# Six-feature groups on two 32-row blocks, and the side matmuls gathered behind every third slot

## The chip, the core and the metric

One core of a Trainium2 chip runs the whole kernel in one launch. The time is device microseconds of an execution; the kernel before takes 6139.32 us (median of 3 runs, 6136.94 to 6142.77).

## The reference, cut to what matters

The input is 8 images of 128 channels on 36 by 36 pixels. A convolutional attention layer is followed by a layer over tokens, of which the costly part is an additive attention: each image has 1296 tokens of 128 features, and every pair of tokens is scored by a sum of 128 hyperbolic tangents.

```python
q = jnp.einsum('bld,ed->ble', x, Wq) + bq
k = jnp.einsum('bld,ed->ble', x, Wk) + bk
t = jnp.tanh(q[:, :, None, :] + k[:, None, :, :])
scores = jnp.einsum('bijd,d->bij', t, w) + bw[0]
attn = jax.nn.softmax(scores, axis=-1)
return jnp.einsum('bij,bjd->bid', attn, x)
```

A mixture of 64 experts with one hidden layer follows, on the 8 best tokens of each expert. Everything is float32.

## The kernel before, in words

**Scores as fractions.** A tangent is written with exponentials, and the fractions of five or six features are brought to one denominator. Numerator and denominator of such a group are then each a dot product over all sign combinations of its features, 32 for a group of five and 64 for a group of six. The kernel holds exponentials of all these combinations for the queries (`qf`, with a plain and a weighted version) and for the keys (`kf`), in `NF` = 8 blocks of 128 partitions: blocks 0 to 3 hold 16 groups of five, 32 partitions each; blocks 4 to 7 hold 8 groups of six, 64 partitions each. `signs` (L524) builds the matrix of signs at the start, on POOL (L532).

**Units and slots.** A unit is one image (8), one chunk of 432 queries (3) and one tile of 128 keys (10, and an eleventh of 16 keys that works in another layout, `REM_SLOTS`). A full unit has 12 slots of two groups each, listed in `SLOTS` (L50): in every three slots, two of five and then one of six. In all there are 2928 slots.

**One slot** makes two tiles of 128 keys by 432 queries of denominators `d` and two of numerators `n`, each by a matmul over the group's partitions (`products`, L939, the matmul at L949). One float32 matmul has two records in the profile. ACT takes the logarithm of both denominators (L972), and after every second slot one exponential of minus that (L975): this makes reciprocals `lq`. DVE multiplies numerators by them (`terms`, L985, the products at L990 to L1003); in slots 2, 5, 8 and 11 (`DVE_PAIRS`, just the slots of six) DVE also adds them up, in place in PSUM, and otherwise POOL adds them (L1012). At a unit's end POOL joins the two sums and ACT takes the exponential of the score (L1032).

**The order of the loop** (L1113 and on) is written out by hand and each engine runs its instructions in it. In turn `p` it issues the numerators of slot `p`, the denominators of slot `p + 3` (`LAG`), the products of slot `p`, and then a turn of other matmuls. A slot of five uses two of the four 32-row quarters of the TensorE array for `n`, and the slot three later uses the other two for `d`; a slot of six uses two 64-row halves for `n` and then the same two for `d`.

**Buffers.** `d` has two buffers of two PSUM banks (`ps_d`). The other four banks (`ps_n`) go round: two for each slot's numerators and one for each step of a side matmul (`aux`). `qf` has 9 buffers (`qfp`).

**Side work.** Everything else (the next image's convolutions, its first attention, tokens, keys; this image's query blocks, its weighted sum, its gates) is written as generators that yield after each step, in four lanes with a precedence: `first_of_all`, `urgent`, `gates`, `background`. A step that issues matmuls is run by `matmul_turn` (L1077) after a slot's own work, one step in a turn, not after slots 1, 4, 7 and 10 except for the first lane, and within a budget of `PACE` = 400 columns for each slot, saved up to two. The instructions that take its result out of PSUM are the generator's next step; `TAKE` lets them be issued by `take_turns` (L1072) in the next turn, outside slots 2, 5, 8, 11 except for the first lane. The next chunk's query blocks are made in the last unit of a chunk, one after each second and third of three slots, in the order `IN_TURN`.

Of the kernel before, what the change touches and what calls it, by code (L numbers as in the profile page):

```python
# [3 lines left out]

# [6 lines left out]
F32 = mybir.dt.float32  # L11
AF = mybir.ActivationFunctionType
ALU = mybir.AluOpType
# [7 lines left out]
CH = 432  # L21
# [24 lines left out]
NF = 8  # L46
FIVES = 4 * 5 * (NF // 2)

SLOTS = []
for m in range(NF // 2):  # L50
    for i in range(2):
        half = (m + i) % 2
        SLOTS.append((m, [slice(64 * half + 32 * h, 64 * half + 32 * h + 32) for h in range(2)]))
    SLOTS.append((NF // 2 + m, [slice(64 * h, 64 * h + 64) for h in range(2)]))
NP = len(SLOTS)
IN_TURN = [m + i for m in range(NF // 2) for i in (0, NF // 2)]
LAG = 3
SHIFT = 6.5
DVE_PAIRS = (2, 5, 8, 11)
PACE = 400  # L60

HALVES = [slice(0, 64), slice(64, 128)]
REM_BANKS = [[(q + i, rows) for i in range(2) for rows in HALVES] for q in (0, 2)]
REM_BANKS.append([(NF // 2 + i, slice(0, 128)) for i in range(4)])
REM_SLOTS = [REM_BANKS[:2], REM_BANKS[2:]]


@with_exitstack  # L70
def kernel(
# [28 lines left out]
    nc = tc.nc  # L100
    mm = nc.tensor.matmul
    ctx.enter_context(tc.manual_schedule())

    const = ctx.enter_context(tc.tile_pool(name="const", bufs=1))
# [25 lines left out]
    with ExitStack() as loop, ExitStack() as score:  # L130
# [20 lines left out]
        ps_n = pool("ps_n", 4, space=bass.MemoryType.PSUM)  # L151
# [19 lines left out]
        def load_raw_taps(w, name):  # L171
# [36 lines left out]
            out=gavg3, in_=gavg3, compare_op=ALU.is_ge, fill=0.0, base=0,  # L208
# [4 lines left out]
            pattern=[[C // G, G], [0, C // G]], channel_multiplier=-1,  # L213
        )

        pairs = const.tile([128, 2, 2], F32, tag="pairs", name="pairs")
        nc.gpsimd.memset(pairs, 0.0)
        for s in range(2):
            nc.gpsimd.memset(pairs[64 * s : 64 * s + 64, 1, s : s + 1], 1.0)
            for o in (32 * s, 64 + 32 * s):  # L220
                nc.gpsimd.memset(pairs[o : o + 32, 0, s : s + 1], 1.0)

        by_key = const.tile([128, 2, REM], F32, tag="by_key", name="by_key")
        for s in range(2):
# [44 lines left out]

        TAKE = (False, 1)

        def step(rest=1):
            return (False, rest)
# [4 lines left out]
        behind = [0]  # L280
# [241 lines left out]
        def signs():  # L522

            sign = big_tile("sign")[:, : NF * 128]  # L524
            nc.gpsimd.memset(sign, 0.0)
            for n, first, half in ((5, 0, sign[:, : NF * 64]), (6, FIVES, sign[:, NF * 64 :])):
                groups = NF * 64 >> n
                for r in range(n):
                    v = half.rearrange("p (g h b l) -> p g h b l", g=groups, b=2, l=2**r)
                    for bit, value in ((0, -1.0), (1, 1.0)):  # L530
                        w = v[:, :, :, bit, :]
                        nc.gpsimd.affine_select(  # L532
                            out=w, in_=w, compare_op=ALU.not_equal, fill=value, base=-first - r,
                            pattern=[[-n, groups], [0, 2 ** (n - 1 - r)], [0, 2**r]],
                            channel_multiplier=1,
                        )
            return sign

        feat = {}
# [127 lines left out]
        def keys(b, tiles):  # L667

            xT = prepared[b][1]
            yield matmuls(1)  # L670
            for t in tiles:
                o, n = KT[t]
                first = (b, t) == (0, order[0])
                if first:
                    kf_of[0] = kfp.tile([128, NF, 128], F32, tag="kf", name="kf")
                for q0 in (0, NF // 2):
                    some = slice(q0, q0 + NF // 2)
                    pk = aux("pk1").rearrange("p (q t) -> p q t", t=128)
                    for q in range(NF // 2):
                        bmm(pk[:, q, :n], a_k[:, (q0 + q) * 128 : (q0 + q + 1) * 128],  # L680
                           xT[:, o : o + n], start=True, stop=True)
                    yield TAKE
                    if first:
                        ks = kf_of[0][:, some, :]
                    else:
                        ks = kstp.tile([128, NF // 2, 128], F32, tag="ks", name="ks")
                    nc.scalar.activation(ks[:, :, :n], pk[:, :, :n], AF.Exp)
                    kd3 = kd[b][t].rearrange("p (q t) -> p q t", t=128)[:, some, :]
                    if n == REM:

                        for x in range(2):
                            nc.gpsimd.tensor_scalar(
                                ks[:, :, (x + 1) * n : (x + 2) * n], ks[:, :, :n],
                                pairs[:, min(q0, 1), x : x + 1], None, ALU.mult,
                            )
                        nc.sync.dma_start(kd3[:, :, : 2 * n], ks[:, :, n : 3 * n])
                    else:
                        nc.sync.dma_start(kd3, ks)
                    if q0 > 0:
                        made.add((b, t))  # L700
                    yield matmuls()
# [209 lines left out]
        def drain(*gens):  # L911
            for g in gens:
                for _ in g:
                    pass
# [6 lines left out]
        slots = []  # L921
# [15 lines left out]
        def new_block(b, c, q):  # L937
            qf = qfp.tile([128, 2, CH], F32, tag="qf", name="qf")
            qf_of[b, c, q] = qf  # L939
            return query_block(b, c, q, qf)  # L940

        def products(u, k, part, outs):

            b, c, j = units[u]
            kf = kf_of[u]
            if j < NKT - 1:
                q, rows = SLOTS[k]
                for h in range(2):
                    mm(outs[h][:, :CH], kf[rows[h], q, :], qf_of[b, c, q][rows[h], part, :],  # L949
                       start=True, stop=True)  # L950
                return
            for out, bank in zip(outs, REM_SLOTS[k]):
                for i, (q, rows) in enumerate(bank):
                    mm(out[32 * i : 32 * i + 32, :CH], kf[rows, q, :32],  # L954
                       qf_of[b, c, q][rows, part, :], start=True, stop=True)

        def banks(u, k):
            return 2 if units[u][2] < NKT - 1 else len(REM_SLOTS[k])

        def denominators(p):  # L960

            if p >= len(slots):
                return
            u, k = slots[p]
            d = ps_d.tile([128, 2, 512], F32, tag="d", name="d")
            n = banks(u, k)
            products(u, k, 0, [d[:, h, :] for h in range(n)])
            if k % 2 == 0:
                lq_of[u, k // 2] = lp.tile([128, 4, CH], F32, tag="lq", name="lq")
            lq = lq_of[u, k // 2]  # L970
            o = 2 * (k % 2)
            nc.scalar.activation(lq[:, o : o + n, :], d[:, :n, :CH], AF.Ln)  # L972
            if k % 2 == 1:
                some = lq[:, : o + n, :]
                nc.scalar.activation(some, some, AF.Exp, scale=-1.0)  # L975

        def numerators(p):
            ns = [ps_n.tile([128, 512], F32, tag="n", name="n") for _ in range(banks(*slots[p]))]
            products(*slots[p], 1, ns)
            return [ps[:, :CH] for ps in ns]  # L980

        def terms(p, ns):

# [90 lines left out]
                if lane.due(p, False) and (k not in DVE_PAIRS or lane is first_of_all):  # L1074
                    lane.run(p)

        def matmul_turn(p, k):  # L1077


            before = behind[0]  # L1080
            for lane in lanes:
                while lane.due(p, True) and behind[0] == before:
                    paced = balance[0] < 0 or k + 1 in DVE_PAIRS
                    if lane is not first_of_all and paced or lane is gates and urgent:
                        break
                    lane.run(p)
            balance[0] = min(balance[0] - (behind[0] - before) + PACE, 2 * PACE)

        drain(normal(0))
        for name in ("wv_t", "wq_t"):  # L1090
# [9 lines left out]
        a_q, a_k, cs_s, fb_s, eb_s = (feat[n] for n in ("a_q", "a_k", "cs_s", "fb_s", "eb_s"))  # L1100
        drain(tokens(0), keys(0, order[:1]))
        for i, q in enumerate(IN_TURN):
            if i < 3:
                drain(new_block(0, 0, q))
            else:
                first_of_all.append(new_block(0, 0, q))
        for p in range(LAG):
            denominators(p)
        drain(keys(0, order[1:3]))
        prefetch(1)  # L1110
        urgent.append(keys(0, order[3:]))
# [1 line left out]
        for p, (u, k) in enumerate(slots):  # L1113
# [12 lines left out]
                             keys(b + 1, range(NKT)))  # L1126
                        )
            take_turns(p, k)
            ns = numerators(p)
            denominators(p + LAG)  # L1130
            terms(p, ns)
            if pending and pending[0][0] <= p:
                exps(p, *pending.popleft()[1:])
            last = p + 1 == len(slots) or slots[p + 1][0] != u

            if j == order[-1] and u + 1 < len(units) and k % 3:
                used = IN_TURN.index(SLOTS[k][0]) + 1
                if used < NF:
                    first_of_all.append(new_block(*units[u + 1][:2], IN_TURN[used]))
            elif j == order[-2] and last and u + 2 < len(units):  # L1140
                first_of_all.append(new_block(*units[u + 2][:2], IN_TURN[0]))
            matmul_turn(p, k)
            if last and rem:
                first_of_all.append(rem_scores(p, u, live.pop("rem")))
            elif last:
# [212 lines left out]
```

The softmax here doesn't subtract the row's maximum and nothing guards it: scores larger than these inputs give would overflow.

## Time and profile before

| what | value |
|---|---|
| median of the runs | 6139.32 us |
| span of the profiled execution | 6139.0 us |
| around the span (median less span) | 0.3 us |
| first and last logarithm (L972) start | 156.2 and 5983.1 us |
| busy share PE, ACT, DVE, POOL | 97, 86, 78, 75% |
| mean granted TensorE clock | 0.985 of full |
| DMA | 270.87 MB, mean 44 GB/s |

A busy share is the time in which an engine has an instruction in flight, over the span. The profile's pages name TensorE as PE for its matmuls and PEld for its weight loads, VectorE as DVE, ScalarE as ACT, GpSimd as POOL. A window's row gives for each engine the busy time and, in brackets, the number of instructions. A timeline row gives the start, the time to the end of the last of the merged instructions, the engine, the line, the operation, what it writes and reads, and rows by columns of the array. The list of waits gives who waited for whom, the sum in us, how often, and the longest.

The work falls into a head (to 156.2 us) that makes the first image's first attention, tokens and first keys; eight batches of 33 units, one for each image, seven of them with the next image's side work; and a tail of experts from 5985 us on.

### The profile page before, as it was taken

Reading aid. Unit: us, or ns where it says so; the run is one execution under the profiler, and the core shown is the slowest. Engines: PE = TensorE matmul, PEld = TensorE weight load, DVE = VectorE, ACT = ScalarE, POOL = GpSimd, SP = SyncE. Lnnn points to the kernel's source line nnn. Section 1 sums busy time; section 2 is a strip of 40 time slices with the busy share of each in tenths; the row PEclk is TensorE's granted clock in tenths of the full one; section 3 lists DMA queues with packets and bytes.
Section 4 is the critical chain, followed back from the end, with each engine's and each line's share of the span. In section 5 each row is a group of like instructions: output and inputs, shape, how many; then the busy total and the mean of one; then the engine's idle time right before and its main releaser. Section 6 shows DMA issues by size and latency. Waiting matters only on the chain.

```text
span 6139.0 us, 93072 instructions
## 1 busy us (share of the span) xinstructions
PE 5957.9 (97%) x33480; PEld 2862.1 (47%) x33480; DVE 4796.4 (78%) x9521; ACT 5279.9 (86%) x5371; POOL 4597.7 (75%) x2819
## 2 busy tenths in 40 slices
PE   7999999999999999999999999999999999999996
PEld 5454444544544445444455444454444544544443
DVE  4787878877788787877888777887778877788882
ACT  1888898888988888889998889888898888999990
POOL 4777777777787777778778786877777777787870
PEclk9999999999999999999999999999999999999997
DMA  1210011100110002100111001110011100110008
GB/s 44 70 37 22 25 62 38 34 25 28 68 43 20 26 27 71 39 24 23 44 55 39 22 24 59 44 39 22 20 65 40 34 25 28 58 50 29 28 20 297
DMA packets 151519, 270.87 MB, mean 44 GB/s; under 512 B 45648, under 2 KB 76752, under 8 KB 151056
## 3 DMA queue, kind: packets, MB, share of 16 engines
q1 hardware_dynamic: 151056, 264.92, 13.0%
q8 instruction: 264, 4.33, 0.3%
q14 instruction: 199, 1.63, 0.1%
HBM read 200.41 MB, written 64.19 MB: 43 GB/s over the span
## 4 chain that ended last, share of the span: by engine, by line
PE 77%; ACT 7%; DVE 6%; issue 6%; POOL 2%; DMA 1%; SPq 0%; DVEq 0%; POOLq 0%; ACTq 0%
PE n L949 37%; PE d L949 12%; PE pa L284 7%; PE pc L284 5%; ACT lq L972 5%; PE s L284 3%; PE pk L284 3%; PE pq L284 3%; DVE rp L1003 2%; DVE n L997 1%; DVE accd L999 1%; PE d L954 1%; ACT lq L975 1%; DMA w<-in_weight_dram 1%; PE n L954 1%
## 5 line engine op out<-in xcount | busy, mean ns | idle before, releaser
L1012 POOL TENSOR_TENSOR accp<-accp,rp 128x864 f32<-128x864 f32 x1440 | 2915.8, 2025 | 1041.0 <-DVE rp L1003 948.8
L949 PE MATMUL n<-qf,kf 32*128 32x432 f32 (+1 forms) x11520 | 3325.3, 574 | 46.5 <-ACT e L1032 13.3
L949 PE MATMUL d<-qf,kf 32*128 32x432 f32 (+1 forms) x11520 | 2991.6, 561 | 38.7 <-ACT lq L972 38.2
L972 ACT ACTIVATE lq<-d 128x864 f32<-128x864 f32 x2928 | 2524.2, 878 | 542.6 <-PE d L949 512.1
L1003 DVE TENSOR_TENSOR rp<-n,lq 128x432 f32<-128x432 f32 x3912 | 2173.3, 600 | 743.5 <-PE d L949 542.8
L975 ACT ACTIVATE lq<-lq 128x1728 f32<-128x1728 f32 (+1 forms) x1464 | 2398.2, 1638 | 46.3
L949 PEld LDWEIGHTS n<-qf,kf 32*128 32x128 f32 (+1 forms) x11520 | 1206.4, 184 | 1600.3 <-DVE rp L1003 581.5
L949 PEld LDWEIGHTS d<-qf,kf 32*128 32x128 f32 (+1 forms) x11520 | 1090.0, 185 | 422.1 <-issue 224.7
L997 DVE TENSOR_TENSOR n<-n,lq 128x432 f32<-128x432 f32 x1440 | 814.9, 608 | 142.1 <-PE n L949 88.5
L999 DVE TENSOR_TENSOR accd<-n,accd 128x432 f32<-128x432 f32 x1440 | 866.3, 602 | 24.6
L1010 POOL TENSOR_TENSOR accp<-rp 128x864 f32<-128x864 f32 x240 | 485.2, 2022 | 197.7 <-DVE rp L1003 195.6
L711 POOL TENSOR_SCALAR qf<-qf,cs_s 128x432 f32<-128x432 f32 x192 | 260.9, 1365 | 45.0 <-ACT qf L710 44.4
L284 PEld LDWEIGHTS pa<-xh,e 128*108 128x108 f32 x1920 | 222.5, 174 | 131.1 <-DVE rp L1003 56.0
L1021 POOL TENSOR_TENSOR accd<-accp,accd 128x432 f32<-128x432 f32 x240 | 265.2, 1105 | 18.8
L1019 POOL TENSOR_TENSOR accp<-accp 128x432 f32<-128x432 f32 x240 | 264.4, 1102 | 16.7
L284 PE MATMUL pa<-xh,e 128*108 128x129 f32 x1920 | 262.9, 283 | 8.7 <-ACT e L1032 5.2
L284 PE MATMUL s<-q,k 128*116 128x432 f32 x480 | 230.3, 568 | 1.7 <-DVE q L316 1.4
L284 PEld LDWEIGHTS pk<-xT,a_k 128*128 128x128 f32 x1408 | 171.2, 192 | 107.0 <-DVE n L997 33.7
L462 POOL TENSOR_TENSOR tot<-tot,e 116x432 f32<-116x432 f32 x192 | 212.0, 1104 | 6.0 <-ACT e L471 4.6
L471 ACT ACTIVATE e<-s 116x432 f32<-116x432 f32 x240 | 124.9, 520 | 98.3 <-PE s L284 97.9
L284 PE MATMUL pa<-e,vw 116*128 116x432 f32 x480 | 204.6, 549 | 0.0
L284 PE MATMUL pk<-xT,a_k 128*128 128x128 f32 (+1 forms) x1408 | 202.5, 287 | 0.1
(213 smaller groups left out, 3788.4 us busy)
## 6 DMA issues: line engine op xcount, KB each, us to landing
kf<-kd SPq DMA_DIRECT2D x239, 512.0 KB
kd<-ks SPq DMA_DIRECT2D x158, 256.0 KB
w<-in_weight_dram SPq DMA_DIRECT2D x32, 1024.0 KB
wk_t<-wk_t_d SPq DMA_DIRECT2D x7, 768.0 KB
wv_t<-wv_t_d SPq DMA_DIRECT2D x7, 768.0 KB
wq_t<-wq_t_d SPq DMA_DIRECT2D x7, 768.0 KB
x<-in_x_dram SPq DMA_DIRECT2D x8, 648.0 KB
t<-tokd SPq DMA_DIRECT2D x96, 54.0 KB
```

The lines of the kernel that those rows point to most:

```text
L284: mm(out, lhsT, rhs, **kw)
L711: nc.gpsimd.tensor_scalar(qf[:, 1, :], qf[:, 0, :], cs_s[:, q : q + 1], None, ALU.mult)
L949: mm(outs[h][:, :CH], kf[rows[h], q, :], qf_of[b, c, q][rows[h], part, :], start=True, stop=True)
L972: nc.scalar.activation(lq[:, o : o + n, :], d[:, :n, :CH], AF.Ln)
L975: nc.scalar.activation(some, some, AF.Exp, scale=-1.0)
L997: mult(ns[h], ns[h], lq[:, o + h, :])
L999: nc.vector.tensor_add(live["d"], ns[h], live["d"])
L1003: mult(rp[:, h, :], n, lq[:, o + h, :])
L1010: nc.gpsimd.tensor_add(live["p"], live["r"], rp)
L1012: nc.gpsimd.tensor_add(live["p"], live["p"], rp)
L1019: nc.gpsimd.tensor_add(s[:, 0, :], s[:, 0, :], s[:, 1, :])
L1021: nc.gpsimd.tensor_add(d, s[:, 0, :], d)
```

## The change

The groups of six keep their 64 sign combinations, but these now lie in two blocks: the 32 combinations of the first five features and a minus sign for the sixth in one block, and those with a plus sign two blocks on, on the same 32 partitions. A slot of six is now four matmuls of 32 rows for `n` and four for `d`, in pairs that accumulate in PSUM, on the same two quarters; and the generators `numerators` and `denominators` are run in rounds, so that two matmuls of `n` and two of `d` follow each other. The line numbers of the changed kernel are 963 for these matmuls and 290 for the side matmuls.

`matmul_turn` gives the paced lanes a turn only after slots 2, 5, 8 and 11, and then runs as many steps as a budget of 355 columns for each slot (saved up to four) allows; `TAKE` becomes (False, 0), and the step that takes a result out is issued at once in the same turn. The first lane may still run after any slot. The next chunk's query blocks are ordered after the new use of blocks and made after slots 2, 5, 8 (two) and 11 (two), the last after slot 2 of the new chunk.

```diff
-    for i in range(2):
-        half = (m + i) % 2
-        SLOTS.append((m, [slice(64 * half + 32 * h, 64 * half + 32 * h + 32) for h in range(2)]))
-    SLOTS.append((NF // 2 + m, [slice(64 * h, 64 * h + 64) for h in range(2)]))
+    for blocks, half in (
+        ((m,), m % 2),
+        ((m,), (m + 1) % 2),
+        ((NF // 2 + m // 2, NF // 2 + 2 + m // 2), m % 2),
+    ):
+        rows = [slice(64 * half + 32 * h, 64 * half + 32 * h + 32) for h in range(2)]
+        SLOTS.append((blocks, rows))
...
-IN_TURN = [m + i for m in range(NF // 2) for i in (0, NF // 2)]
+IN_TURN = [0, 4, 6, 1, 2, 3, 5, 7]
+NEXT_AT = {2: (4,), 5: (6,), 8: (1, 2), 11: (3, 5)}
+TURNS = (2, 5, 8, 11)
...
-PACE = 400
+PACE = 355
...
-REM_BANKS.append([(NF // 2 + i, slice(0, 128)) for i in range(4)])
+REM_BANKS.append([
+    ((NF // 2 + m, NF // 2 + 2 + m), rows) for m in range(2) for rows in HALVES
+])
...
-        TAKE = (False, 1)
+        TAKE = (False, 0)
...
-                q, rows = SLOTS[k]
-                for h in range(2):
-                    mm(outs[h][:, :CH], kf[rows[h], q, :], qf_of[b, c, q][rows[h], part, :],
-                       start=True, stop=True)
+                blocks, rows = SLOTS[k]
+                for q in blocks:
+                    for h in range(2):
+                        mm(outs[h][:, :CH], kf[rows[h], q, :],
+                           qf_of[b, c, q][rows[h], part, :],
+                           start=(q == blocks[0]), stop=(q == blocks[-1]))
+                    yield
                 return
...
+        def in_rounds(*gens):
+            for _ in zip_longest(*gens):
+                pass
...
-            before = behind[0]
-            for lane in lanes:
-                while lane.due(p, True) and behind[0] == before:
-                    paced = balance[0] < 0 or k + 1 in DVE_PAIRS
+            balance[0] = min(balance[0] + PACE, 4 * PACE)
+            while True:
+                for lane in lanes:
+                    paced = not turn or balance[0] < 0
                     if lane is not first_of_all and paced or lane is gates and urgent:
+                        continue
+                    if lane.due(p, True):
                         break
+                else:
+                    return
+                before = behind[0]
+                lane.run(p)
+                balance[0] -= behind[0] - before
+                while lane.due(p, False):
                     lane.run(p)
-            balance[0] = min(balance[0] - (behind[0] - before) + PACE, 2 * PACE)
...
-            ns = numerators(p)
-            denominators(p + LAG)
-            terms(p, ns)
+            ns = []
+            in_rounds(numerators(p, ns), denominators(p + LAG))
+            terms(p, [ps[:, :CH] for ps in ns])
...
-            matmul_turn(p, k)
+            matmul_turn(p, k == 1 if rem else k in TURNS)
```

`signs` builds the second half of its matrix in two parts of five bits and a constant sixth, 32 selects on POOL in place of 22, the new ones for the sixes mostly on half as many elements. The multiplies, logarithms, exponentials and additions of the loop, and its transfers, are the same in number and size.

## The prediction

> **What bounds the kernel now.** I read the page first, its busy shares and its costliest groups.
>
> ```profile
> PE 5957.9 (97%) x33480; PEld 2862.1 (47%) x33480; DVE 4796.4 (78%) x9521; ACT 5279.9 (86%) x5371; POOL 4597.7 (75%) x2819
> ...
> L972 ACT ACTIVATE lq<-d 128x864 f32<-128x864 f32 x2928 | 2524.2, 878 | 542.6 <-PE d L949 512.1
> L1003 DVE TENSOR_TENSOR rp<-n,lq 128x432 f32<-128x432 f32 x3912 | 2173.3, 600 | 743.5 <-PE d L949 542.8
> L975 ACT ACTIVATE lq<-lq 128x1728 f32<-128x1728 f32 (+1 forms) x1464 | 2398.2, 1638 | 46.3
> ```
>
> PE is at 97%, but four matmuls in flight count like one, so that says little. ACT is next: a slot costs it 0.88 us of logarithm and half of 1.64 us of exponential. It idled 512 us for denominators from PE: PE was late for it.
>
> Then windows: a unit of the last batch without side matmuls, the fifth batch, the last batch, and the whole loop. Columns are PE, PEld, DVE, ACT, POOL, clock, DMA.
>
> ```profile
> 5923.00:5943.00 20.00, 19.24 (x96) 7.67 (x96) 16.77 (x33) 19.81 (x21) 16.41 (x10) 1.00 0.12 39
> 3109.50:3846.50 737.00, 726.82 (x4083) 348.45 (x4082) 594.42 (x1180) 659.33 (x671) 570.65 (x347) 0.99 0.12 37
> 5324.40:5985.00 660.60, 639.89 (x3594) 288.19 (x3588) 548.17 (x1071) 617.71 (x605) 526.38 (x297) 1.00 0.10 32
> 155.00:5985.00 5830.00, 5733.46 (x32138) 2722.65 (x32137) 4686.91 (x9260) 5238.31 (x5307) 4512.22 (x2711) 0.99 0.11 37
> ```
>
> Without side work a unit takes 20 us with ACT 99% busy: ACT bounds it. In a full batch ACT is at 659.3 of 737 us, 89.5%. So **PE bounds the batches that carry side work**, and ACT is the floor just below.
>
> Last, PE's timeline in a stretch almost without side work.
>
> ```profile
> 3005.19 0.63 PE L949 MATMUL n<-qf,kf 32*128 32x432 f32 x2
> 3005.20 0.63 PE L949 MATMUL d<-qf,kf 32*128 32x432 f32 x2
> 3005.66 0.53 PE L949 MATMUL n<-qf,kf 32*128 32x432 f32 x2
> 3005.67 0.53 PE L949 MATMUL d<-qf,kf 32*128 32x432 f32 x2
> 3006.03 0.53 PE L949 MATMUL n<-qf,kf 32*128 32x432 f32 x2
> 3006.24 0.63 PE L949 MATMUL d<-qf,kf 32*128 32x432 f32 x2
> 3006.40 0.53 PE L949 MATMUL n<-qf,kf 32*128 32x432 f32 x2
> 3006.71 0.53 PE L949 MATMUL d<-qf,kf 32*128 32x432 f32 x2
> 3007.17 1.22 PE L949 MATMUL n<-qf,kf 64*128 64x432 f32 x4
> 3008.70 1.00 PE L949 MATMUL d<-qf,kf 64*128 64x432 f32 x4 [0.31 <-ACT lq L972]
> ```
>
> Two `n` and two `d` of 32 rows start within 0.01 us of each other, and the next pass of `n` comes 0.37 us later (5.66, 6.03, 6.40), four in the time of one. Where it begins anew the step is 0.47 us (5.19 to 5.66), and so it is from 32 to 64 rows (6.71 to 7.17): a change of form shows about 0.1 us of weight load that is hidden otherwise.
>
> **The change part by part.** *Matmuls of the sixes.* Before, a slot of six is eight records of 64 rows, two at a time: four passes. After, sixteen of 32 rows, four at a time: four passes, 4 x 0.37 = 1.5 us. The loop issues 4,032 more matmuls and PE gains or loses nothing if the passes fill; the slow rival below prices the case that they don't.
>
> *Changes of form.* In the built order of TensorE's instructions side matmuls interrupt the slots 1,489 times before, 752 behind a slot of five (two changes added), 730 behind a six (one added), above the 8 in every one of 240 units: 1,920 + 1,504 + 730 = some 4,150. After it is 832 interruptions with two each and none between fives and sixes: 1,660. 2,490 x 0.1 = 249 us leave PE.
>
> *Waits for PSUM.* Before, a step after almost every slot took one of the four banks, so the next slot's second `n` needed a bank of the slot just before. PE's weight loads of `n` waited 581.5 + 198.5 + 92.0 us for DVE's L1003, L999 and L997 in the list of waits. Now two slots in three have no step behind them, and most of this goes. Together these exceed what ACT allows, so **ACT's floor decides**: I sum from there and add what still holds ACT up.
>
> *Floor.* The first seven batches run from 156.2 to 5324.4 us, 738.3 each. ACT is busy (5238.3 - 617.7)/7 = 660.1 us in each, and at the 99% of the bare unit that is 666.8.
>
> *The turn's new wait.* Several steps now stand on PE in front of the next slot, and take two or more banks. Take an odd slot of six (5 or 11) and count from the end of its pair's exponential. ACT: logarithms of slots 6 and 7 to 1.76, exponential to 3.40, logarithm of 8 to 4.28, then it wants `d` of 9. PE: `d` of 8 gets its buffer at 0.88 and is done at 2.4; `n` of 5 is done by about 1.8. DVE: slot 4 to 1.2, then slot 5's four operations of 0.6 from 1.8 to 4.2; its first bank is free after the third, 3.6, the second at 4.2. A turn of one step leaves `n` of 6 one of these banks to wait for: start 3.65, `d` of 9 done at 4.5, ACT 0.25 late. After two or more steps both are needed: start 4.25, done at 5.1, 0.85 late. Of the 832 turns 425 have one step, so 0.55 on the mean. Behind an even six (2 or 8) the same count has `d` ready by 4.8 and wanted at 5.04: nothing. A full batch has 111 turns, 47% behind odd sixes: 52 x 0.55 = 28.8 us. The trace of before has no such turn, so both ends stay: 0, and 0.85 at all 52 odd turns with 0.25 at the 59 even ones, 59 us. The mean of the counted steps is nearest to the rows.
>
> *Units that DVE bounds.* The windows of two units with the gates' wide operations show DVE, not PE or ACT:
>
> ```profile
> 3163.10:3187.10 24.00, 22.33 (x115) 10.45 (x112) 22.06 (x46) 20.20 (x21) 18.59 (x10) 0.93 0.12 41
> 3187.10:3209.00 21.90, 21.53 (x122) 10.80 (x124) 21.31 (x46) 20.24 (x20) 17.20 (x11) 1.00 0.07 18
> ```
>
> At 99% of ACT they would be 20.4 each; I keep 3.6 + 1.5 = 5.1 us in every full batch.
>
> *Sum.* A full batch: 666.8 + 28.8 + 5.1 = 700.7, 37.6 less than 738.3; seven make 263. The last: 617.7/0.99 = 623.9, and 55 turns x 0.47 x 0.55 = 14.2, so 638.1 for 660.6: 22.5.
>
> *The rest.* `signs` lies on the head's chain: 22 selects take 24.1 us (0.52 to 2.2 each), the sixes' 12 of them 12.3. Two parts of half the elements cost between nothing more and 13 us; I take 2. Its cover would be PE's convolutions, which is thin. Moved steps issue the same DMAs in bunches on SP's queue, a key tile's load is asked for two units (some 44 us) ahead, and the DMA engines are 10% busy: nothing. Two query blocks in one turn put two 1.37 us multiplies in a row on POOL, ahead of a 2.02 us addition; POOL is at 77% in the loop: nothing, at most 1.4 us in each of 24 chunks. Results now taken out in the same turn stand on DVE and ACT behind the slot's own work; PE finishes them by then, so nothing, and if not it is in the wait above.
>
> 6139.0 - 263 - 22.5 + 2 = 5855.5 for the profiled execution, and with the 0.3 us around it 5856, against the median of 6139.3.
>
> **A rule against the change.** Four passes in flight show 0.37 us against 0.36 for a full-array matmul of the same 432 columns, as good as fourfold. The Trainium skill, "TensorE: Matmul & The Clock Gate", Part 3 ("Measured speedup vs the span model"), gives four row tiles of 32 a measured 3.07 times. By it a six's sixteen records would take 16 x 0.36/3.07 = 1.9 us, 0.4 more than above in 960 slots, an estimate of 380 us that would eat the gain. The rows here decide for 0.37.
>
> **The rivals.** *ACT alone bounds it.* The new wait is hidden by the two `d` buffers: 666.8 + 5.1 in seven batches, 623.9 in the last: 6139.3 - 465 - 37 + 2, some 5640. For it: the bare unit's 99%, and side work now evenly spread. Against it: the count above.
>
> *The turn gives it back.* The wait costs 0.85 at odd sixes: 716.1 a batch, 5971 in all; with 0.25 at even ones 730.9 a batch, 6079. For it: DVE is at 80% in the loop and takes side results out in bunches.
>
> *Slower: `n` held behind `d`.* In a six's rounds the second block of `n` stands behind the first `d`, which waits for ACT. Passes that miss each other are seen: above, `d` at 6.24 came 0.2 us behind `n` at 6.03, and that slot took 7.17 - 6.03 = 1.14 us for 0.74. If both halves of a six ran so it would take 2.3 for its 1.83 now (with its change of form): 0.47 x 960 = 450 us more, less the 249 saved: 6340. It decides from 1.83 + 0.26 = 2.1 us a six. Against it: where `d` waits for ACT, ACT is busy and PE is not the bound.
>
> *It does nothing.* Where the waits of PE are ACT's and DVE's in disguise, the time stays: 6139.
>
> **Chances.** The forecast, 5856 (5750 to 5960), 0.60; ACT alone 0.18; given back 0.10; nothing 0.03; slower 0.09. About 0.2% is what a measurement of this kernel can tell from no change; so faster 0.88, same 0.03, slower 0.09. The range runs from 5640, the second case, through the forecast to 6000, a little past the milder price of the third, which leaves out 0.19.
>
> **What would show it.** ACT's busy share of a full batch rising from 89.5% to about 94%; records of a six starting in fours 0.37 us apart; interruptions by side matmuls only behind sixes, their first load 0.1 us exposed; the 872 us of `n` loads waiting for DVE falling by more than half, what is left sitting behind turns; ACT's wait for `d`, 512 us, falling but not to nothing. Wrong if a six takes over 2.1 us, if ACT is idle for 0.8 us at every turn, or if DVE passes ACT in share.

## The result: 4.6% slower, and the profile after

The changed kernel takes 6420.87 us (median of 4 runs, 6407.26 to 6423.48) against 6138.30 for the kernel before (6136.94 to 6142.77): ratio 1.0456 [1.0441, 1.0471], 282 us slower. The forecast was 5856 and the range ended at 6000. The profiled execution took 6407.26 us with a span of 6405.5, 266.5 longer than before's. Head and tail hold almost none of that: the first logarithm starts at 159.5 us (156.2 before), and from the loop's end to the end are 154 us in both. The loop grew from 5830 to 6092 us.

From the page, the busy shares and the three groups that the prediction began with (L991, L1026 and L994 were L972, L1003 and L975):

```profile
PE 6118.1 (96%) x41544; PEld 3371.1 (53%) x41544; DVE 4802.7 (75%) x9521; ACT 5271.6 (82%) x5371; POOL 4604.2 (72%) x2827
...
L991 ACT ACTIVATE lq<-d 128x864 f32<-128x864 f32 x2928 | 2491.6, 878 | 812.0 <-PE d L963 728.1
...
L1026 DVE TENSOR_TENSOR rp<-n,lq 128x432 f32<-128x432 f32 x3912 | 2134.6, 599 | 603.1 <-PE d L963 280.9
L994 ACT ACTIVATE lq<-lq 128x1728 f32<-128x1728 f32 (+1 forms) x1464 | 2398.0, 1638 | 46.4
```

ACT does the same work in the same time. Its idle time before the logarithms went from 542.6 to 812.0 us, 269 more: about as much as the loop grew. It is PE that is late with `d`, 728.1 us for 512.1.

The windows, in the prediction's order (a unit without side matmuls, the fifth batch, the last batch, the loop; PE, PEld, DVE, ACT, POOL, clock, DMA):

```profile
5980.30:6000.30 20.00, 19.25 (x130) 10.01 (x129) 16.89 (x31) 19.81 (x21) 16.32 (x9) 1.00 0.09 27
3243.70:4015.80 772.10, 747.16 (x5092) 410.19 (x5089) 594.41 (x1180) 657.20 (x671) 571.02 (x346) 0.99 0.11 36
5558.60:6251.50 692.90, 662.14 (x4623) 351.33 (x4617) 552.86 (x1070) 621.10 (x609) 530.42 (x300) 0.99 0.10 31
159.50:6251.50 6092.00, 5890.50 (x40188) 3229.90 (x40188) 4692.98 (x9260) 5228.44 (x5304) 4514.61 (x2710) 0.99 0.11 36
```

The bare unit still takes 20 us with ACT at 99%. The batches with side work moved away from that floor, not towards it: the fifth takes 772.1 us for 737.0, ACT's share fell from 89.5 to 85.1%, where the prediction wanted 94%.

From the list of waits (columns: us in total, how often, longest):

```profile
ACT lq L991 <- PE d L963: 728.1, 659, 4.0
PEld n L963 <- DVE rp L1026: 558.6, 1429, 1.7
PEld n L963 <- DVE accd L1022: 314.4, 687, 1.8
...
DVE n L1020 <- PE n L963: 268.6, 433, 3.7
```

PE's loads of `n` still wait for DVE, 558.6 + 314.4 + 22.8 (behind L1020, further down the list) = 896 us for 872. And the other way DVE now waits for PE's `n`: 268.6 here, 201.3 and 76.4 at L1026 and L1015, 546 us for 159 before. Part of that is a change of what comes last: DVE's waits for `d` at the products of L1026 fell from 542.8 to 280.9. What a six looks like, from PE's timeline (start, us to the last end, operation, records merged):

```profile
3434.26 1.14 PE L963 MATMUL n<-qf,kf 32*128 32x432 f32 x3
3434.79 0.63 PE L963 MATMUL d<-qf,kf 32*128 32x432 f32 x2
3435.09 0.68 PE L963 MATMUL n<-qf,kf 32*128 32x432 f32 x2
3435.26 0.53 PE L963 MATMUL d<-qf,kf 32*128 32x432 f32 x2
3435.46 0.68 PE L963 MATMUL n<-qf,kf 32*128 32x432 f32 x2
3435.62 0.53 PE L963 MATMUL d<-qf,kf 32*128 32x432 f32 x2
3435.97 0.52 PE L963 MATMUL n<-qf,kf 32*128 32x432 f32 x1
3435.98 0.53 PE L963 MATMUL d<-qf,kf 32*128 32x432 f32 x2
```

Four passes of 0.37 were to make 1.5 us. Here only the first of the two banks of `n` starts at 34.26, and its last records end up beside the last `d`: with a last pass of 0.36 the slot takes 2.08 us. The weight loads in front of these matmuls show what held the rest:

```profile
3434.26 0.29 PEld L963 LDWEIGHTS n<-qf,kf 32*128 32x128 f32 x2 [0.61 <-DVE rp L1026]
3434.78 0.18 PEld L963 LDWEIGHTS n<-qf,kf 32*128 32x128 f32 x1 [0.23 <-DVE rp L1026]
3434.79 0.19 PEld L963 LDWEIGHTS d<-qf,kf 32*128 32x128 f32 x2
```

The second bank of `n` waited for DVE 0.52 us longer than the first, and `d`, which the program puts behind it, follows at once. Two products of DVE that follow each other start 0.52 us apart (the median of L1026). This is the most common case: of 935 sixes (those whose `d` is of a full unit too) 452 have the second bank of `n` more than 0.2 us behind the first and `d` within 0.03 us of that. In 61 only `d` is late, in 86 both are. Over these sixes, from the first record's start to the last one's plus 0.36, the mean went from 1.86 to 2.14 us and the median from 1.73 to 2.08 (the expectations below go by a first count, 1.85 and 2.10); `d` starts 0.52 after the first `n` in the median.

The late second bank is not new: before, too, it came 0.27 us behind the first on the mean (0.37 after), and more than 0.2 us in 404 of the 935. But there `d` had only to be ready when `n` had run. Now the later of the second bank and `d` starts 0.56 us after the first `n` on the mean, 0.29 more than the second bank did before, and the six has grown by 0.28.

The same starts tell how full the array was. A record of 432 columns counts for 0.36 us (fewer columns in proportion), on a quarter of the array for 32 rows, on half for 64 and on all of it above. Of the loop, before and after: idle 1000 and 886 us, full 3353 and 3065, half or three quarters full 1128 and 1326, a quarter 349 and 815. So idle time did leave (114 us), and 664 us of partly empty time came. PE's busy share, 97 and 96%, shows none of it.

The granted clock fell too, from 0.985 to 0.979. The traces' clock record has the loop at half clock for 88.7 us before and 167.3 after, and there the two passes of a five's `n` start 0.88 and 0.72 us apart (medians of 9 and 22 fives), for 0.47 outside. If the array had set the pace in all of these stretches, the difference would have cost half of itself, 39 of the 282 us: an estimate, and an upper bound.

### The profile page after: what moved, and what is told of

Same layout as the page of the kernel before. It is cut to its first block, busy times and chain, and to the rows that moved or that the text cites. A ratio compares the mean times of both kernels' runs of the same rounds, so it can differ in the third digit from the quotient of the medians.

```text
span 6405.5 us, 110416 instructions
## 1 busy us (share of the span) xinstructions
PE 6118.1 (96%) x41544; PEld 3371.1 (53%) x41544; DVE 4802.7 (75%) x9521; ACT 5271.6 (82%) x5371; POOL 4604.2 (72%) x2827
## 4 chain that ended last, share of the span: by engine, by line
PE 72%; ACT 9%; DVE 8%; issue 7%; POOL 2%; DMA 1%; SPq 0%; DVEq 0%; POOLq 0%; ACTq 0%
PE n L963 39%; PE d L963 10%; PE pa L290 6%; ACT lq L991 6%; PE pc L290 5%; PE s L290 3%; PE pq L290 2%; PE pk L290 2%; DVE rp L1026 2%; DVE accd L1022 2%; DVE n L1020 2%; ACT lq L994 1%; PE d L971 1%; PE n L971 1%; DMA w<-in_weight_dram 1%
## 5 line engine op out<-in xcount | busy, mean ns | idle before, releaser
L963 PE MATMUL n<-qf,kf 32*128 32x432 f32 x15360 | 4061.1, 556 | 126.1 <-DVE accd L1022 40.4
L963 PE MATMUL d<-qf,kf 32*128 32x432 f32 x15360 | 3459.0, 565 | 32.2 <-ACT lq L991 28.7
L991 ACT ACTIVATE lq<-d 128x864 f32<-128x864 f32 x2928 | 2491.6, 878 | 812.0 <-PE d L963 728.1
L963 PEld LDWEIGHTS n<-qf,kf 32*128 32x128 f32 x15360 | 1937.0, 186 | 1684.6 <-DVE rp L1026 558.6
L1026 DVE TENSOR_TENSOR rp<-n,lq 128x432 f32<-128x432 f32 x3912 | 2134.6, 599 | 603.1 <-PE d L963 280.9
L994 ACT ACTIVATE lq<-lq 128x1728 f32<-128x1728 f32 (+1 forms) x1464 | 2398.0, 1638 | 46.4
L963 PEld LDWEIGHTS d<-qf,kf 32*128 32x128 f32 x15360 | 1285.5, 186 | 305.1 <-ACT lq L991 183.6
L1020 DVE TENSOR_TENSOR n<-n,lq 128x432 f32<-128x432 f32 x1440 | 814.2, 611 | 434.8 <-PE n L963 268.6
L1015 DVE TENSOR_TENSOR accd<-n,lq 128x432 f32<-128x432 f32 x240 | 145.8, 608 | 155.0 <-PE n L963 76.4
L290 PE MATMUL s<-q,k 128*116 128x432 f32 x480 | 206.9, 548 | 1.4 <-DVE q L322 1.4
```

What stands on the lines that cost most here:

```text
L290: mm(out, lhsT, rhs, **kw)
L1020: mult(ns[h], ns[h], lq[:, o + h, :])
L1026: mult(rp[:, h, :], n, lq[:, o + h, :])
```

## The experiments

The theories at the start: the sixes share the array badly (*sixes*), or the turns of several steps hold up what follows them (*turns*). Timed runs are medians of 4, or of 10 in one case, each beside the kernel before on the same chip.

**Each half by itself.** The kernel before with the new turns, old sixes:

```diff
+NEXT_AT = {2: (4, 1), 5: (5, 2), 8: (6, 3), 11: (7,)}
+TURNS = (2, 5, 8, 11)
-PACE = 400
+PACE = 355
-        TAKE = (False, 1)
+        TAKE = (False, 0)
... matmul_turn and its call as in the change
```

> The sixes as before (64 rows, n then d), the turns of the changed kernel (only behind sixes, several steps, 355 columns a slot). Theory of half-filled passes: a six on four quarters is full only when n and d start together, and they don't (2.10 us a six in the changed kernel's trace against 1.85 before); so the loss of 960 x 0.25 = 240 us goes, a third change of form comes back in every three slots (960 x 0.1 = 96 us): some 6180 to 6270. Rival, the turns: several steps in a turn make the next slot wait for PSUM banks and ACT for d; the loss stays, 6380 or more.

6237.0 us, 1.0158 [1.0141, 1.0175]: 98 slower. And the changed kernel with the old `matmul_turn`:

```diff
-PACE = 355
+PACE = 400
-        TAKE = (False, 0)
+        TAKE = (False, 1)
... matmul_turn and its call as before
```

> The sixes of the changed kernel (two blocks on 32 rows, n and d in rounds), the turns of the kernel before (one step after two slots in three, 400 columns a slot); query blocks are asked for in the changed kernel's order. Half-filled passes: 6138 + 240, less the 1190 changes of form between fives and sixes that had no step between them (119 us): some 6260, or above if the fives suffer too. Turns as the cause: 6138 - 119, some 6020.

6390.9 us, 1.0413 [1.0397, 1.0428]: 252 slower, and 130 above the 6260 that the theory of the half-filled passes gave for unharmed slots of five. Both halves lose; the sixes are the larger, and their granted clock was that of before (0.985).

Both halves save changes of form too. In the order of the records in the traces the loop has, without those at the short units of 16 keys, 4,228 of them before, 3,128 with the sixes alone, 2,887 with the turns alone and 1,785 with both. By the prediction's 0.1 us for each (an estimate) the sixes save 110 us and the turns 134, so their gross costs are some 360 and 230 us. These savings add up (1,100 and 1,341 to 2,443). The times don't: the halves make 350 and the whole is 282, so it is the losses that overlap. How was not tried.

The gross cost of the sixes is not all in the slot itself. With the sixes alone a six takes 1.98 us (1.86 in the median), 0.12 more than before, in 960 slots some 115 us; a five, measured in the same way, takes 1.16 for 1.06 (0.093 more), in 1,920 slots some 180 us.

**Is it ACT that holds `d`?** In both kernels the logarithm becomes a copy of the same size and the exponential a copy of 8 of 432 columns:

```diff
-            nc.scalar.activation(lq[:, o : o + n, :], d[:, :n, :CH], AF.Ln)
+            nc.scalar.activation(lq[:, o : o + n, :], d[:, :n, :CH], AF.Copy, scale=0.0)
-                some = lq[:, : o + n, :]
-                nc.scalar.activation(some, some, AF.Exp, scale=-1.0)
+                some = lq[:, : o + n, :8]
+                nc.scalar.activation(some, some, AF.Copy, scale=0.0)
```

> The kernel before with ACT relieved: the logarithm is a copy times zero of the same size, and the exponential is one on 8 of 432 columns, so that all scores are equal and the result is not the reference's. d then hardly waits for ACT. Both theories: faster than 6138; PE or DVE bounds it, 5400 to 5800. It is the base for the next run.

> The changed kernel with ACT relieved in the same way (logarithm a copy times zero, exponential on 8 of 432 columns; the scores are all equal). Half-filled passes: with d no longer late the sixes fill, 1.6 us each, and the saved changes of form show: 100 to 250 us faster than the run before. Turns as the cause: the banks are freed by DVE, not ACT, so it stays slower than the run before by 100 or more.

5916.6 before, 6114.1 after (one execution each, as in all runs of this kind): still 198 slower, with ACT far from the bound (58 and 56% busy). A six took 1.72 and 2.00 us. The second bank of `n` came 0.51 us behind the first in the median, as DVE frees them, and in 600 of the 935 sixes `d` right behind it.

**Is it DVE that holds `n`?** As above, and DVE's work on the sixes left out but for one product in each unit:

```diff
-                    mult(ns[1], ns[1], lq[:, o + 1, :])
-                    nc.vector.tensor_add(live["d"], ns[1], live["d"])
-                else:
-                    for h in range(2):
-                        mult(ns[h], ns[h], lq[:, o + h, :])
-                    for h in range(2):
-                        nc.vector.tensor_add(live["d"], ns[h], live["d"])
```

> The kernel before with ACT relieved as above and DVE too: of the products and additions of slots 2, 5, 8 and 11 only the first product of a unit is left (15 of 16 left out), so banks of the sixes come free at once; the result is not the reference's. Base for the next run: some 5500 to 5800.

> The changed kernel with ACT and DVE relieved in the same way (logarithm a copy times zero, exponential on 8 of 432 columns, 15 of 16 operations of the sixes on DVE left out). If a six on four quarters is only spoilt by operands that come free one after the other (n's second bank 0.52 us after its first, in the run with ACT alone relieved), most sixes now take 1.56 us and this run is 100 to 250 us faster than the one before it. If the array doesn't carry the accumulating quarters at 0.37 us a pass, or the turns cost by themselves, it stays slower by 100 or more.

5780.8 and 5905.3: 125 slower. The six stayed at 2.03 us, with `d` 0.52 behind the first `n`, in 763 of 935 right behind a late second bank: these banks are those of the slot two before, a five, and DVE still frees them one by one.

**Where the turns stand.** ACT's idle time before its logarithms, by slot, had grown at slots 3 and 9 of the turns-only kernel (352 us in both, 158 before), which come behind the turns of 11 and 5. *Theory of the pair*: a turn behind an odd slot hits the pair that is about to take its exponential. The turns-only kernel with even turns, then odd ones:

```diff
-NEXT_AT = {2: (4, 1), 5: (5, 2), 8: (6, 3), 11: (7,)}
-TURNS = (2, 5, 8, 11)
+NEXT_AT = {2: (4, 1), 4: (5,), 6: (2,), 8: (6, 3), 10: (7,)}
+TURNS = (0, 2, 4, 6, 8, 10)
```

```diff
+NEXT_AT = {1: (4,), 3: (1,), 5: (5, 2), 7: (6,), 9: (3,), 11: (7,)}
+TURNS = (1, 3, 5, 7, 9, 11)
```

> Sixes as before; side matmuls behind the even slots 0, 2, 4, 6, 8, 10, several steps in a turn, 355 columns a slot. Theory of the pair: ACT takes two logarithms and then one exponential of 1.64 us, so the denominators of an odd slot are wanted 3.4 us after those of the even one could start; a turn behind an odd slot stands just between the two (six 1.5, turn 1.85, five 0.75: 4.1 us), one behind an even slot falls in time in which PE would wait for a buffer anyway. Then ACT's idle time at slots 3 and 9 (352 us in the run with the turns only) goes: 5980 to 6080. Rival, that several steps in any one place hold up PSUM: 6200 or more.

> The same with the turns behind the odd slots 1, 3, 5, 7, 9, 11. Theory of the pair: every turn stands between two denominators of one pair; 6250 to 6400. Rival (several steps anywhere): like the run with even slots within 50 us.

Even: 6279.0, 1.0230 [1.0215, 1.0245]. Odd: 6226.0, 1.0140 [1.0123, 1.0157]. The theory fell: the odd turns are the better ones, by 53 us. With even turns the idle time at slots 3 and 9 did go, from 352 to 96 us, and came back at others: 646.8 us in all against 657.1.

**Both engines out of the way.** As in the pair of DVE, and nearly all products of DVE and additions of POOL in the loop on 8 of 432 columns:

```diff
-                    mult(rp[:, h, :], n, lq[:, o + h, :])
+                    mult(rp[:, h, :8], n[:, :8], lq[:, o + h, :8])
...
-                    nc.gpsimd.tensor_add(live["p"], live["p"], rp)
+                    nc.gpsimd.tensor_add(live["p"][:, :, :8], live["p"][:, :, :8], rp[:, :, :8])
```

> The kernel before with ACT relieved as above, and nearly all of DVE's and POOL's work on the scores left out: one product of a unit is whole, the others and POOL's additions cover 8 of 432 columns (the short unit of 16 keys keeps its products). PE then hardly waits for banks or denominators. Base for the next: 4900 to 5500.

> The changed kernel relieved in the same way. Theory of the spread: the four quarters of a six carry at 0.37 us a pass, and are spoilt only because their operands come free one after the other; with nothing to wait for the sixes take 1.5 to 1.6 us and the 249 us of saved changes of form show, 150 to 250 us faster than the run before it. Rival, the array or its order of issue: sixes stay at 2 us and this run is as slow or slower.

5485.2 and 5597.4: 112 slower, a six 1.60 and 1.91 us. PE's timeline of the bare kernel before, one six:

```profile
2502.80 1.00 PE L949 MATMUL n<-qf,kf 64*128 64x432 f32 x4
2503.63 0.89 PE L949 MATMUL d<-qf,kf 64*128 64x432 f32 x4
```

The two `n` of 64 rows fill the whole array for 0.83 us, and only then does `d` begin. The bare changed kernel:

```profile
2506.06 0.89 PE L963 MATMUL n<-qf,kf 32*128 32x432 f32 x4
2506.53 0.63 PE L963 MATMUL d<-qf,kf 32*128 32x432 f32 x2
2506.79 0.53 PE L963 MATMUL n<-qf,kf 32*128 32x432 f32 x2
2506.99 0.53 PE L963 MATMUL d<-qf,kf 32*128 32x432 f32 x2
2507.15 0.53 PE L963 MATMUL n<-qf,kf 32*128 32x432 f32 x2
2507.36 0.89 PE L963 MATMUL d<-qf,kf 32*128 32x432 f32 x4
```

`n` starts at once, both banks, and uses half of the array; `d` comes 0.47 us later (0.45 in the median), since the logarithm, still of 0.88 us, holds its buffer. Here, with DVE at 24%, that is the common case: `d` alone is late in 697 of the 935 sixes. From then on the two alternate, and the last pass of `d` stands by itself. This gave the *theory of the cover*: in the old form `n` covers 0.83 us of waiting for `d`'s buffer with a full array, in the new form nothing does. It says more than the others: with `d`'s buffers free at once the changed kernel must be the faster one.

**The cover made needless.** The logarithm too on 8 of 432 columns, in both kernels (and the one whole product of each unit's sixes becomes a multiply of `n` by zero, with 8 columns of the product):

```diff
-            nc.scalar.activation(lq[:, o : o + n, :], d[:, :n, :CH], AF.Copy, scale=0.0)
+            w = CH if units[u][2] == NKT - 1 else 8
+            nc.scalar.activation(lq[:, o : o + n, :w], d[:, :n, :w], AF.Copy, scale=0.0)
```

> As the bare kernel before, and ACT's logarithm too covers 8 of 432 columns (the short unit of 16 keys stays whole), so that denominators' buffers come free at once. Base for the next: 5200 to 5450.

> The changed kernel relieved in the same way. In the bare run of the changed kernel n of a six started at once and d 0.45 to 0.52 us later, waiting for its buffer; in the old form n's 0.83 us on the whole array lie over that wait. Theory of the cover: with buffers free at once the sixes take 1.5 to 1.6 us and this run is 150 to 250 us faster than the run before it. Rival, order of issue or the array: sixes stay near 1.9 us and it is no faster.

5407.0 and 5119.9 us: the changed form is 287 us *faster*. A six takes 1.58 and 1.56 us, and idle time of the array in the loop fell by 396 us (814 to 418). A six of the changed one:

```profile
2459.94 0.88 PE L963 MATMUL n<-qf,kf 32*128 32x432 f32 x4
2460.30 0.53 PE L963 MATMUL d<-qf,kf 32*128 32x432 f32 x2
2460.65 0.53 PE L963 MATMUL n<-qf,kf 32*128 32x432 f32 x2
2460.67 0.53 PE L963 MATMUL d<-qf,kf 32*128 32x432 f32 x2
2461.01 0.53 PE L963 MATMUL n<-qf,kf 32*128 32x432 f32 x2
2461.03 0.53 PE L963 MATMUL d<-qf,kf 32*128 32x432 f32 x2
2461.38 0.53 PE L963 MATMUL n<-qf,kf 32*128 32x432 f32 x2
2461.39 0.53 PE L963 MATMUL d<-qf,kf 32*128 32x432 f32 x2
```

The first row holds two records of the five before and the first two `n` of the six, which start at 60.29 and 60.30, together with the first two `d`. From there all go on at 0.36 to 0.37 us (60.65, 61.01, 61.38): the passes fill, as the prediction priced them. Sixes like this one are 252 of the 935. In most of the others `n` and `d` start up to 0.2 us apart, but each keeps this rate: the median from the first to the last start of `n`, three steps, is 1.09 us.

Between the two pairs one logarithm's length changed (and one product in a unit), and the sign with it. The sums nearly close: in the first pair 960 sixes x 0.31 us less the 244 us of 2,443 changes of form make 54 us slower (112 measured), in the second 960 x -0.02 less 244 make 263 us faster (287). What stays open is each hold by itself in the real kernel: no run shortens the logarithm alone, and none issues all of `n` before `d` in the new form.

**What it is in the turns.** *Theory of the pace*: side work that ends sooner would help. One edit, in the turns-only kernel, the changed kernel and the kernel before:

```diff
-PACE = 355
+PACE = 450
```

(In the kernel before, 400 becomes 450.)

> The run with the turns only, but with 450 columns a slot in place of 355. Theory of the pace: a unit with side work takes some 24.5 us almost whatever its amount, and 355 columns spread it over more units; finished earlier it leaves more units at 20 us: 6150 to 6190. Rival (several steps in a turn hurt by themselves): more steps to a turn, 6237 or slower.

> The changed kernel with 450 columns a slot in place of 355. Pace: 6330 to 6370. Rival (several steps in a turn): 6420 or slower.

> The kernel before with 450 columns a slot in place of 400. More pace cost 113 us with several steps in a turn; with one step the load cannot bunch within a turn, only over a unit. If bunching in the turn is what pace costs, within 30 us of the kernel before, either way; if more side work in a unit costs by itself, 6200 or more.

6351.1, 1.0352 [1.0335, 1.0369]; 6450.3, 1.0510 [1.0494, 1.0526]; 6184.2, 1.0078 [1.0063, 1.0093]. It fell: each kernel gets slower, by 114, 29 and 48 us (each less its own form at the lower pace). The last falls between its two expectations. So side work that stands denser costs, in the old turns too: for each column of pace 1.2 us with the turns alone, 0.3 in the changed kernel and 1.0 in the kernel before. At the same pace of 450 the turns alone are 167 us slower than the old turns.

Then the number of steps. The turns-only kernel with at most one step in a turn, at eight slots and `PACE` 400; and with at most two, at `PACE` 450:

```diff
-TURNS = (2, 5, 8, 11)
-PACE = 355
+TURNS = (0, 2, 3, 5, 6, 8, 9, 11)
+PACE = 400
...
-            balance[0] = min(balance[0] + PACE, 4 * PACE)
-            while True:
+            balance[0] = min(balance[0] + PACE, 2 * PACE)
+            steps = 0
+            while steps < 1:
...
+                steps += behind[0] > before
```

```diff
-PACE = 355
+PACE = 450
...
-            while True:
+            steps = 0
+            while steps < 2:
```

> Sixes as before; the changed kernel's way of a turn (results taken out at once, query blocks two at a time) but behind the same eight slots as in the kernel before, 400 columns a slot, and at most one step in a turn. If several steps are what costs in the turns, this is within 20 us of the kernel before, 6120 to 6160. If taking the results out at once costs, 6190 or more.

> The run with the turns only, behind sixes, with at most two steps in a turn and 450 columns a slot: 816 turns, none with three steps or more (the run with 450 columns and no cap has 687, 181 of them with three or more, and took 6351). Theory: from the third step a turn needs a bank of its own six, which DVE frees only with its third operation of 0.6 us, and PE stands still in order: 6160 to 6220. Rival, any second step costs alike: 6240 or more.

One step: 6192.2, 1.0087 [1.0071, 1.0104], 53 slower than before. Two: 6308.6, 1.0273 [1.0258, 1.0289], 170 slower. The cap gave back 43 of 6351.1, so it is not only the third step that costs. Last, the order of the next chunk's query blocks alone, two in a turn, in the kernel before:

```diff
+NEXT_AT = {2: (4, 1), 5: (5, 2), 8: (6, 3), 11: (7,)}
...
+                for q in NEXT_AT.get(k, ()):
+                    first_of_all.append(new_block(*units[u + 1][:2], q))
```

> The kernel before, with only the next chunk's query blocks asked for two at a time behind the sixes, as in the run with one step in a turn (6192). If the query blocks are the 53 us of that run, 6175 or more; if results taken out at once are, within 15 us of the kernel before.

6151.6, 1.0023 [1.0014, 1.0033]: 15 us.

The clock moved along with the turns. The mean granted clock was 0.978 with the turns alone, 0.986 with one step in a turn and 0.985 before; at half clock the loop spent 180.9, 81.9 and 88.7 us. Half of the difference between the first two, some 50 us, is the most that this can have cost (an estimate), and it is as much as the 45 us between these two runs. No run holds the clock and changes the turns.

No run that does the same work beats the kernel before. A form that frees `d`'s buffers earlier with the same work was not tried.

## Why the prediction was wrong, point by point

**The step that failed: "four passes, 4 x 0.37 = 1.5 us. ... PE gains or loses nothing if the passes fill".** They don't. A six takes 2.14 us for 1.86, and the sixes alone cost 252 us net. The rate was right: 0.36 to 0.37 us a pass in the barest kernel. What was missing is that in the new form both banks of `n` and the buffer of `d` (of the slot three later) must be free together, where before two matmuls of either filled the array by themselves. They are not: DVE frees the two banks of `n` 0.52 us apart, and `d` stands behind the second one; with that out of the way ACT's logarithm holds `d`. Shown: with both holds taken away the changed kernel is 287 us faster; with DVE's alone taken away (and ACT's exponential cut short, as in all these pairs) 112 slower. What goes on from there is read in the traces, not tried by itself: `n`'s records of a six spread over 1.97 us in place of 1.10, DVE waits for `n` 546 us in place of 159 (and less for `d`), so banks and then `d` come late, fives take longer, and ACT idles 269 us more.

**"Slower: `n` held behind `d`" was the nearest of the rivals,** at 6340, and its threshold of 2.1 us a six was met. It had the order the wrong way round: in the most common case `d` is held, behind a second bank of `n` that DVE frees late, which the rival left out. That its price is near is in part luck. By that price a six of 2.14 less the saved changes of form comes out some 50 us slower; the turns, and the fives and slots behind a six, make up the rest. The reason given against the rival, "where `d` waits for ACT, ACT is busy and PE is not the bound", does not cover a `d` that waits for DVE: ACT's idle time before its logarithms grew from 542.6 to 812.0 us.

**Changes of form, 249 us: right in kind.** The trace's records give 2,443 fewer of them, 244 us by the same price. Idle time of the array fell by 114 us in the loop, and by 396 between the barest pair; both sums hold other waits as well. What was saved was paid back elsewhere.

**"Most of this goes" (872 us of `n` loads waiting for DVE): wrong.** It is 896 us. It falls neither with the turns alone (763.8 + 228.8 for the two largest of these waits there) nor in the whole. The count looked only at the bank that a side step takes; that DVE, kept waiting for `n`, frees the others later is argued from the 546 us, not tried.

**"ACT's floor decides": wrong, as a consequence.** It held on the bare unit alone (20 us, ACT at 99%).

**The turn's new wait, 0.55 us at turns behind 5 and 11: right in place, too small.** In the changed kernel ACT idles 454 us at slots 3 and 9, over 480 of them 0.95 each; with old sixes 352 us, 0.73 each. Against 158 us before, the turns-only kernel has 194 us there and gets 80 back at other slots (657.1 - 542.6 = 114 in all); the prediction charged it and then let ACT's floor absorb everything else. The 98 us are net of some 134 saved in changes of form, and part of them may be the clock's. Some 15 of them are the query blocks (by itself), some 40 the rest of the one-step run, results taken out in the same turn above all (53 - 15, by subtraction), and some 45 the gathering into turns behind sixes (98 - 53, the same), net of all of the 134. How these act on each other stays open, and the lower pace of 355 was not tried alone in the old form of turns. A small slip: the higher price of "the turn gives it back" adds up to 6082, not 6079.

**The head: 3.3 us for 2.** The 5.1 us of units that DVE bounds were not tested.

**The rule weighed against the change.** The rows decided for 0.37, and the six with both products ready, 1.56 us, bears that out. The Trainium skill, "TensorE: Matmul & The Clock Gate", Part 3 ("Measured speedup vs the span model"), would have made it 1.9 by its 3.07 times, an estimate of 380 us more. The gross cost found, some 360, comes near that estimate by another way, waiting rather than rate: no run here shows four filled quarters at 3.07 times.

## What to carry to other kernels

Where several matmuls share the array, ask when each of them becomes ready: independent products in one pass only fill it if their buffers come free together, and a matmul that fills the array alone is cover for the wait of the next. A busy share of 96% on TensorE says nothing on this; records' starts, counted by how much of the array they use, do. And work spread as one step behind each slot is worth something by itself: the new turns cost 98 us here, though they save changes of form, and 167 us at the denser pace. Look at the granted clock of such runs before putting all of that down to waits.

## What the runs showed of the chip

Four accumulating matmuls of 32 rows ran in passes of 0.36 to 0.37 us, the same as one full-array matmul of 432 columns (0.36), when all were ready. A half-microsecond lag of one pair at a slot's start was not made up within the slot: `n` and `d` went on alternating about 0.2 us apart, to the end (6.79, 6.99, 7.15, 7.36 above). And relieving two of three engines left the wait for the third: with DVE and POOL at 20 to 25%, one logarithm of 0.88 us behind two `d` buffers still went with a six of 1.91 us for 1.60. At half of the granted clock the two passes of a five's `n` started 0.88 us apart for 0.47 (kernel before, medians of 9 fives and of the others), and the loops with several steps in a turn behind sixes spent about twice as long at half clock as the loop before (167.3 and 180.9 us for 88.7).
